# First-lane rows gathered two experts ahead, parts of an expert scattered without order, conditional rows gathered at the head of their block

## The chip, the core and the metric

The kernel runs on one core of a Trainium2 chip. The time is microseconds on the device for one execution. The engines of the core are TensorE (PE: matrix products and transposes), VectorE (DVE), ScalarE (ACT), GpSimd (POOL), which also issues the indirect transfers, and SyncE (SP), which issues the weight loads. Each has its own queue of instructions, and they wait for each other and for transfers by semaphores.

## The reference

One transformer layer on 2048 tokens of width 512, in float32: linear attention with a causal running state (16 heads, 4 key heads), then a mixture of experts. Only the experts matter here.

```
logits = xf @ w_cls.T;  scores = softmax(logits)            # 64 choices, 32 of them experts
topk_idx = top_k(scores + bias, 8)
w = 1.5 * scores[topk_idx] / sum(scores[topk_idx])
buf[e, pos] = xf of the tokens that chose expert e           # at most 256 for each
g, u = split(buf @ w_gate_up[e])                             # 512 -> 2 x 256
y = (silu(g) * u) @ w_down[e]                                # 256 -> 512
out[token] = sum over its experts of w * y                   # and a factor for the other choices
x = x + out
```

## The kernel before

**Attention.** Four blocks of 512 tokens. As each chunk of 128 tokens is finished, it is written to the output (`out<-x`), and its normalized row with its 32 expert weights to a table in memory, `rows`. `route` finds the eight choices, and `list_further` writes token numbers into `slots` by indirect transfers.

**Places.** `place` sorts the experts by the number of their tokens so far into eight groups of four. The eight fullest are the first lane of the groups: numbers 0, 4, 8, ..., 28. Rank r and place are tied by `place_of`.

**Three kinds of expert work.** A token list is cut at 32 and at 160 rows.

- *Groups.* The first 32 rows of the four experts of a group are one tile of 128 rows (`xg_b`). `group_up(q)` forms the gate and up products (L722), `group_down(q)` the down product (L739, `y_b` at L742), then a product that adds up equal rows (L744) gives `z` (L746), which is scattered.
- *First lane.* `over(4q, ...)` treats the next 128 rows (`xg_o`) and the last 96 rows (`xg_t`) of the group's first expert always: transposes (L708), gate and up products (L765), `aT` (SiLU on ScalarE L768, product on VectorE L769), down product (L778), and the weighted rows `y` (first part on ScalarE L786, second on VectorE L784). `weight` finds each row's weight on VectorE (`one` L687, `w` L689) from the gathered row itself.
- *Further experts.* After the last group, `further(r)` goes through the other ranks as nested blocks that run only while a flag says that the rank has more than 32 rows; a second flag adds 96 rows (`xg_r`).

**Gathers and scatters** are indirect transfers issued by GpSimd: `gather` (L675) takes rows by index from `rows`; `scatter` (L694) adds rows of 2 KB to the output. `tc.chain_iter_dep("out", ...)` puts every scatter in one chain. GpSimd issues a scatter of the chain when the one before has landed, and what stands behind it in GpSimd's queue waits as well.

**The loop over the groups:**

```
    gather_first(0)
    for q in range(NQ):
        if q + 1 < NQ:
            gather_first(q + 1)
        over(Q * q, [(xg_o[q % 2], P), (xg_t[q % 2], M2)])
        ...group_down(q), group_up(q + 1), two weight loads
```

`load_pair` loads the weights of two experts (3 MB) five pairs ahead, on SyncE, into buffers that come free when the products of earlier experts are done.

**Order.** The instructions are written for a scheduler that decides the order on each engine when the program is built, from its own estimate of when each operand is there; the order is then fixed. `tc.issue_after` keeps what it encloses behind one instruction on that engine's queue. The buffers of a tile (`bufs`) bound how far the scheduler can bring work forward.

Of the kernel before, what the change touches and what calls it, by code (L numbers as in the profile page):

```python
# [9 lines left out]
F32 = mybir.dt.float32  # L10
# [8 lines left out]
P = 128  # L19
S = 2048  # L20
# [9 lines left out]
E = 32  # L30
# [3 lines left out]
Q = 4  # L34
NQ = E // Q
# [11 lines left out]
XW = D + E  # L47
LATE = NQ - 2
# [19 lines left out]
def linattn_moe(  # L68
# [15 lines left out]
    nc = tc.nc  # L84
# [91 lines left out]
    def load_pair(i):  # L176

        home = units if i % 5 < 3 else more_units[0]
        tag = "unit" if home is units else "more"
        vs = [nc.values_load(eids[0:1, n : n + 1], engines=[mybir.EngineType.SP], min_val=0, max_val=E - 1,  # L180
                             skip_runtime_bounds_check_because="places hold a permutation of the experts")
              for n in (2 * i, 2 * i + 1)]
        for n, v in zip((2 * i, 2 * i + 1), vs):
            gu = home.tile([P, KD, 2, FI // P, P], F32, tag=tag, name=f"gu_{n}")
            nc.sync.dma_start(out=gu.rearrange("p k a c f -> p k (a c f)"),
                              in_=wgu[bass.ds(v, 1)].rearrange("e (k p) f -> p (e k) f", p=P))
            weights[n] = gu
        dn = home.tile([P, 2, FI // P, D], F32, tag=tag, name=f"dn_{i}")
        for j, v in enumerate(vs):
            nc.sync.dma_start(out=dn[:, j], in_=wdn[bass.ds(v, 1)].rearrange("e (k p) f -> p (e k) f", p=P))  # L190
            weights[2 * i + j] = weights[2 * i + j], dn[:, j]

    def list_further(ch, ai):

# [11 lines left out]
    with ExitStack() as ph:  # L206
# [335 lines left out]
        for sb in range(NSB):  # L542
            last = sb == NSB - 1
            if not last:
                blocks[sb + 1] = load_block(sb + 1)
            for g in range(G):
                if g == 0:
                    vas = [values(sb, c, xTs[sb]) for c in range(NC)]
                if g + 1 < G:
                    projs[sb, g + 1] = project(sb, g + 1, xTs[sb])  # L550
                elif not last:
                    xTs[sb + 1] = norm_block(sb + 1)
                    projs[sb + 1, 0] = project(sb + 1, 0, xTs[sb + 1])
                if last and g == 1:
                    rank_e = place()
                if last and g == G - 1:
                    for i in range(2):
                        load_pair(i)
                oT = otp.tile([P, R, SB], F32, tag="oT", name=f"oT_{sb}_{g}")
                oTs[sb, g] = oT  # L560
                for c in range(NC):
                    attend(sb, g, c, projs[sb, g], vas[c], oT)
                    if g == G - 1:
                        if c != 1 and waiting:
                            route_and_list(*waiting.pop(0))
                        if c >= 1:
                            waiting.append((sb * NC + c - 1,
                                            output(sb, c - 1, [oTs[sb, i] for i in range(G)])))
            listed = []
            if last:  # L570
                rows_so_far()
            xw = output(sb, NC - 1, [oTs[sb, i] for i in range(G)],
                        (lambda: listed.append(route(*waiting.pop(0)))) if last else None)
            with tc.issue_after(rstd_of.last.ins):
                for one in listed:
                    list_further(*one)
            while waiting:
                route_and_list(*waiting.pop(0))
            if last:
                route(sb * NC + NC - 1, xw)  # L580
            else:
                waiting.append((sb * NC + NC - 1, xw))
# [47 lines left out]
    def more(i, r):  # L630

        return (words[2 * i + r // 16] >> (r % 16)) & 1


    xg_b = [xgp.tile([P, XW], F32, name=f"xg_b{i}") for i in range(NQ)]
    xg_o = [xgp.tile([P, XW], F32, name=f"xg_o{i}") for i in range(2)]
    xg_t = [xgp.tile([P, XW], F32, name=f"xg_t{i}") for i in range(2)]
    xg_n = [xgp.tile([P, XW], F32, name=f"xg_n{i}") for i in range(3)]
    xg_r = xgp.tile([P, XW], F32, name="xg_r")
    for t in xg_o + xg_t + xg_n + [xg_r]:  # L640
        nc.scalar.mul(t, ident[:, 0:1].to_broadcast([P, XW]), 0.0)

    nc.vector.scalar_tensor_tensor(idx_f, held[:, :, 1], float(P), held[:, :, 0], ALU.mult, ALU.add)
# [27 lines left out]
    def column(n, i):  # L671
        return idx[:, i * E + n : i * E + n + 1]
# [11 lines left out]
    def weight(xg, k, what, of, name):  # L684

        one = xep.tile([P, E], F32, tag="one", name=f"one_{name}")
        nc.vector.scalar_tensor_tensor(one[:k], what, of, xg[:k, D:], ALU.is_equal, ALU.mult)  # L687
        w = xep.tile([P, 1], F32, tag="w", name=f"w_{name}", bufs=4)
        nc.vector.tensor_reduce(w[:k], one[:k], AX.X, ALU.add)  # L689
        return w  # L690

    def scatter(y, i):

        one = nc.gpsimd.indirect_dma_start(  # L694
            out=out,
            out_offset=bass.IndirectOffsetOnAxis(ap=i, axis=0),
            in_=y,
            in_offset=None,
            bounds_check=S - 1,
            oob_is_err=False,  # L700
            compute_op=ALU.add,
        )
        tc.chain_iter_dep("out", one.ins)

    def transposed(n, xg, xeT, m):
        pt = q_tr.tile([P, KD, P], F32, tag="tr", name=f"pe_{n}")
# [24 lines left out]
    def group_down(q, acts):  # L731
        py = q_y.tile([P, D], F32, tag="y", name=f"py_b{q}")
        for c, act in enumerate(acts):
            pa = q_ta.tile([P, P], F32, tag="ta", name=f"pa_{q}_{c}")
            nc.tensor.transpose(pa, act, ident)
            aT = xep.tile([P, P], F32, tag="aT_b", name=f"aT_b{q}_{c}")
            nc.scalar.copy(aT, pa)
            for j in range(Q):
                nc.tensor.matmul(py[ts(j, SL), :], lhsT=aT[:, ts(j, SL)], rhs=weights[Q * q + j][1][:, c, :],  # L739
                                 start=(c == 0), stop=(c == NF - 1))  # L740
        y = yp.tile([P, D], F32, tag="y_b", name=f"y_b{q}", bufs=2)
        nc.vector.tensor_copy(y, py)  # L742
        ps = q_y.tile([P, D], F32, tag="y", name=f"ps_{q}")
        nc.tensor.matmul(ps, lhsT=same[:, q, :], rhs=y, start=True, stop=True)  # L744
        z = yp.tile([P, D], F32, tag="z", name=f"z_{q}", bufs=2)
        nc.scalar.copy(z, ps)  # L746
        scatter(z, idx_s[:, q : q + 1])


    def over(e, parts):  # L750
# [24 lines left out]
        for c in range(NF):  # L775
            at = 0
            for py, (xg, k) in zip(pys, parts):
                nc.tensor.matmul(py[:k, :], lhsT=aTs[c][:, at : at + k], rhs=weights[e][1][:, c, :],  # L778
                                 start=(c == 0), stop=(c == NF - 1))
                at += k  # L780
        for i, (py, (xg, k)) in enumerate(zip(pys, parts)):
            y = yp.tile([P, D], F32, tag="y", name=f"y_{n}_{i}")
            if i:
                nc.vector.tensor_scalar(y[:k], py[:k], ws[i][:k], None, ALU.mult)  # L784
            else:
                nc.scalar.mul(y[:k], py[:k], ws[i][:k])  # L786
            scatter(y[:k], column(e, i)[:k])

    for i in range(2, AHEAD_W):
        load_pair(i)  # L790
# [24 lines left out]
    nc.vector.tensor_copy(idx, pi)  # L815

    def gather_first(q):
        gather(xg_o[q % 2], column(Q * q, 0), S)
        gather(xg_t[q % 2], column(Q * q, 1), S)

    def number_of(r):
        q, j = place_of(r)
        return Q * q + j

    def gather_rank(r):
        gather(xg_n[r % 3], column(number_of(r), 0), S)

    def reload(n, r):

# [8 lines left out]
    def further(r):  # L838

        n = number_of(r)  # L840
        with tc.If(more(0, r)):  # L841
            if n // Q < LATE:
                reload(n, r)
            with tc.If(more(1, r)) as cond:  # L844
                gather(xg_r, column(n, 1), S)
                over(n, [(xg_n[r % 3], P), (xg_r, M2)])
            with cond.Else():
                over(n, [(xg_n[r % 3], P)])
            if r + 3 < E:
                gather_rank(r + 3)  # L850
            if r + 1 < E:
                further(r + 1)

    gather_first(0)
    for q in range(NQ):
        if q + 1 < NQ:
            gather_first(q + 1)
        over(Q * q, [(xg_o[q % 2], P), (xg_t[q % 2], M2)])
        if ahead:
            group_down(q, ahead)  # L860
            ahead = None
        if FIRST <= q + 1 < NQ:
            ahead = group_up(q + 1)
        for i in range(2 * q, 2 * q + 2):
            if i + AHEAD_W < E // 2:
                load_pair(i + AHEAD_W)
# [54 lines left out]
```

## Time and profile before

| what | value |
|---|---|
| three timed runs, median | 1152.19 us (1149.51 to 1156.85) |
| the profiled execution, its own time | 1156.0 us |
| span of the profiled execution | 1154.3 us |
| mean granted TensorE clock | 0.96 |
| busy: TensorE, VectorE, ScalarE, GpSimd | 1036.8, 608.4, 209.8, 229.5 us |
| gathers xg_o and xg_t, each | 8 |
| gathers xg_n (further experts) | 6, of which three were used |
| scatters of y, of z | 19, 8 |
| start of the down product of experts 8, 12, 16, 20, 24, 28 | 992.12, 1017.79, 1042.55, 1066.52, 1089.57, 1108.17 us |
| last scatter, last gather | 1138.32, 1141.01 us |

The span runs from the first to the last instruction; the execution's own time adds what lies around it. "Granted clock" is the share of full speed that TensorE was given. A line of the timeline gives the start, the duration, the engine, the source line, the operation, out<-in, the count, and in brackets the engine's idle time just before with what ended it. An indirect transfer's duration on GpSimd is the time to issue it; it lands later, and the landing is seen where another instruction waits for it.

### The profile page before, as it was taken

The numbers are of one execution on the slowest core, as the hardware profiler recorded it, in microseconds if no ns is written. First come the engines' busy times: TensorE is split into PE (matmuls) and PEld (weight loads), VectorE is DVE, ScalarE is ACT, GpSimd is POOL, SyncE is SP. The second block draws the span as 40 slices with busy tenths as digits, with TensorE's granted clock in tenths as the row PEclk, the third lists the DMA queues.
The fourth block names the chain that finished last, engine by engine and source line by source line (L and its number), as shares of the span: only waits on it lengthen the run. The fifth ranks groups of instructions, "written<-read, shape, count | busy, mean of one in ns | idle before, by whom it ended". The sixth has DMA issues, their size and how long they took to land. (4 is left out here: it accounts for less than half of the span.)

```text
span 1154.3 us, 12767 instructions
## 1 busy us (share of the span) xinstructions
PE 1036.8 (90%) x4420; PEld 585.2 (51%) x4420; DVE 608.4 (53%) x1661; ACT 209.8 (18%) x543; POOL 229.5 (20%) x290
## 2 busy tenths in 40 slices
PE   6999899999998999999899999999897468888883
PEld 3455455544556554456455544556543326455452
DVE  4778874337885832678765426776434322222220
ACT  1122221001223200122222001223101010111110
POOL 6000000530000052300003331000241634222322
PEclk9999999999999999999999999999898588899997
DMA  9400000010000000100000000041004776999210
GB/s 349 151 1 1 18 1 10 30 65 0 1 8 12 11 29 19 56 1 1 1 1 20 29 29 0 1 182 37 19 30 144 289 242 187 344 321 331 27 20 6
DMA packets 51805, 87.25 MB, mean 76 GB/s; under 512 B 11342, under 2 KB 11470, under 8 KB 51728
## 3 DMA queue, kind: packets, MB, share of 16 engines
q1 hardware_dynamic: 35248, 67.31, 16.3%
q0 software_dynamic: 10720, 10.08, 4.1%
q10 hardware_dynamic: 5760, 8.92, 2.1%
q8 instruction: 38, 0.62, 0.2%
q14 instruction: 39, 0.32, 0.1%
HBM read 75.92 MB, written 15.88 MB: 80 GB/s over the span
## 5 line engine op out<-in xcount | busy, mean ns | idle before, releaser
L378 PE MATMUL px<-wo,oT 128*128 128x512 f32 x512 | 234.4, 602 | 0.0
L320 PE MATMUL pq<-xT,wq 128*128 128x512 f32 x512 | 230.5, 595 | 0.5 <-DVE rb_q L302 0.4
L196 POOL DMA_INDIRECT slots<-tok,ai x120 | 117.4, 979 | 242.5 <-DVE ai L478 210.2
L320 PEld LDWEIGHTS pq<-xT,wq 128*128 128x128 f32 x512 | 93.4, 191 | 106.6 <-issue 91.8
L378 PEld LDWEIGHTS px<-wo,oT 128*128 128x128 f32 x512 | 94.4, 194 | 97.7 <-issue 97.5
L342 PE MATMUL po<-va,at 128*128 128x129 f32 x512 | 99.5, 280 | 12.1 <-DVE at L335 11.8
L351 ACT ACTIVATE osb<-po,den 128x128 f32<-128x128 f32 x256 | 77.9, 365 | 152.0 <-DVE den L349 85.7
L342 PEld LDWEIGHTS po<-va,at 128*128 128x128 f32 x512 | 80.1, 193 | 35.7 <-DVE at L335 21.9
L345 PE MATMUL po<-state,qT 128*128 128x129 f32 x480 | 93.7, 277 | 0.0
L291 POOL MEMSET va<- 128x4 f32 x16 | 1.5, 110 | 415.5 <-PE pst L358 415.5
L345 PEld LDWEIGHTS po<-state,qT 128*128 128x128 f32 x480 | 73.6, 194 | 1.3 <-DVE state L361 0.8
L367 PE MATMUL pot<-ident,osb 128*128 128x128 f32 x256 | 60.7, 301 | 15.0 <-ACT osb L351 13.8
L305 ACT ACTIVATE rb_q<-rb_q 128x512 f32<-128x512 f32 x64 | 40.3, 630 | 179.3 <-DVE rb_q L304 164.1
L381 DVE TENSOR_TENSOR x<-px,xs 128x512 f32<-128x512 f32 x16 | 11.1, 692 | 108.9 <-PE px L378 60.6
L333 PE MATMUL psc<-qT,kT 128*128 128x512 f32 x128 | 68.2, 615 | 0.0
L367 PEld LDWEIGHTS pot<-ident,osb 128*128 128x128 f32 x256 | 35.9, 145 | 63.1 <-ACT osb L351 50.2
L765 PE MATMUL pu<-xeT,gu 128*128 128x224 f32 (+1 forms) x352 | 63.3, 339 | 3.9 <-DVE xeT L709 3.9
L765 PEld LDWEIGHTS pu<-xeT,gu 128*128 128x128 f32 x352 | 60.0, 194 | 6.0 <-ACT y L786 2.2
L313 PE MATMUL pk<-xT,wk 128*128 128x512 f32 x128 | 61.1, 614 | 0.8 <-ACT xT L280 0.7
L335 DVE TENSOR_TENSOR at<-psc,causal 128x512 f32<-128x512 f32 x64 | 44.0, 687 | 32.0 <-PE psc L333 31.9
L368 DVE COPY oT<-pot 128x512 f32<-128x512 f32 x64 | 43.9, 686 | 26.1 <-PE pot L367 26.0
L288 PE MATMUL pv<-wv,xT 128*128 128x512 f32 x128 | 57.0, 595 | 0.0
(223 smaller groups left out, 1207.5 us busy)
## 6 DMA issues: line engine op xcount, KB each, us to landing
gu<-in_wgu_dram SPq DMA_DIRECT2D x32, 1024.0 KB
dn<-in_wdn_dram SPq DMA_DIRECT2D x32, 512.0 KB
rows<-xw ACTq DMA_DIRECT2D x16, 272.0 KB
wq<-in_wqT_dram SPq DMA_DIRECT2D x4, 1024.0 KB
wo<-in_woT_dram SPq DMA_DIRECT2D x4, 1024.0 KB
out_dram<-x ACTq DMA_DIRECT2D x16, 256.0 KB
xs<-in_x_dram SPq DMA_DIRECT2D x3, 1024.0 KB
slots<-tok,ai POOLq DMA_INDIRECT x120
```

Source lines behind the costliest of these rows:

```text
L196: nc.gpsimd.indirect_dma_start(out=slots[k][:, :], out_offset=bass.IndirectOffsetOnAxis(ap=ai[:, k : k + 1], axis=0), in_=tok[:, ch : ch + 1],
L288: nc.tensor.matmul(pvf, lhsT=xT[:, k, ts(c, P)], rhs=wv[:, k, :], start=(k == 0), stop=(k == KD - 1))
L313: nc.tensor.matmul(pk, lhsT=wk[:, k, ts(g, HD)], rhs=xT[:, k, :], start=(k == 0), stop=(k == KD - 1))
L320: nc.tensor.matmul(pq, lhsT=wq[g][:, k, ts(r, HD)], rhs=xT[:, k, :], start=(k == 0), stop=(k == KD - 1))
L333: nc.tensor.matmul(psc, lhsT=kT[:, cc], rhs=qT[:, :, cc], start=True, stop=True)
L335: nc.vector.tensor_tensor(at, psc, causal.unsqueeze(1).to_broadcast([P, R, P]), ALU.mult)
L342: nc.tensor.matmul(po[:, i, :], lhsT=at[:, r, :], rhs=va[:, g, :], start=True, stop=(old is None))
L345: nc.tensor.matmul(po[:, i, :], lhsT=qT[:, r, cc], rhs=old, start=False, stop=True)
L351: nc.scalar.mul(osb[:, 2 * j + i, :], po[:, i, :HD], den[:, i : i + 1])
L367: nc.tensor.transpose(pt[:, r, :], osb[:, r, :], ident)
L378: nc.tensor.matmul(px, lhsT=oTs[h // R][:, h % R, ts(c, P)], rhs=wo[h // R][:, h % R, :], start=(h == 0), stop=(h == H - 1))
L765: nc.tensor.matmul(pu[:, a, :m], lhsT=weights[e][0][:, k, a, c, :], rhs=xeT[:, k, :m], start=(k == 0), stop=(k == KD - 1))
```

## The change

First-lane rows are gathered two groups ahead into three buffers. The two parts of a first-lane expert are collected and scattered together: both are made to wait for the scatters written before them, and not for each other; further experts keep the chain. Each conditional block gathers the rows of the rank three further on at its head and not at its end; two of the first-lane buffers serve there as the third and fourth buffer, and one as `xg_r`. The tile `w` has eight buffers in place of four. `rows_so_far` is queued behind the first weight loads.

```diff
-                    for i in range(2):
-                        load_pair(i)
+                    loaded = [load_pair(i) for i in range(2)][-1]
...
-                rows_so_far()
+                with tc.issue_after(loaded.ins):
+                    rows_so_far()
...
-    xg_o = [xgp.tile([P, XW], F32, name=f"xg_o{i}") for i in range(2)]
-    xg_t = [xgp.tile([P, XW], F32, name=f"xg_t{i}") for i in range(2)]
-    xg_n = [xgp.tile([P, XW], F32, name=f"xg_n{i}") for i in range(3)]
-    xg_r = xgp.tile([P, XW], F32, name="xg_r")
+    xg_o = [xgp.tile([P, XW], F32, name=f"xg_o{i}") for i in range(3)]
+    xg_t = [xgp.tile([P, XW], F32, name=f"xg_t{i}") for i in range(3)]
+    xg_n = [xgp.tile([P, XW], F32, name=f"xg_n{i}") for i in range(2)]
...
-        w = xep.tile([P, 1], F32, tag="w", name=f"w_{name}", bufs=4)
+        w = xep.tile([P, 1], F32, tag="w", name=f"w_{name}", bufs=8)
...
-    def scatter(y, i):
-
+    written = []
+
+    def scatter(ys, apart=True):
+        ones_ = [add_rows(y, i) for y, i in ys]
+        for one in ones_:
+            if not apart or not written:
+                tc.chain_iter_dep("out", one)
+            if apart:
+                for name in written:
+                    tc.add_manual_dep(one, name, mybir.DependencyInfo(mybir.DependencyClass.Sync,
+                                                                      mybir.DependencyReason.DATA),
+                                      reason="rows of the output are added to in turn")
+        written[:] = [one.name for one in ones_]
+        return ones_
+
+    def add_rows(y, i):
         one = nc.gpsimd.indirect_dma_start(
...
-        tc.chain_iter_dep("out", one.ins)
+        return one.ins
...
-            scatter(y[:k], column(e, i)[:k])
+            ys.append((y[:k], column(e, i)[:k]))
+        scatter(ys, e % Q == 0)
...
-        gather(xg_o[q % 2], column(Q * q, 0), S)
-        gather(xg_t[q % 2], column(Q * q, 1), S)
+        gather(xg_o[q % 3], column(Q * q, 0), S)
+        gather(xg_t[q % 3], column(Q * q, 1), S)
+
+    xg_n += [xg_o[LATE - 1 - 3], xg_t[LATE - 1 - 3]]
+    xg_r = xg_o[LATE - 6]
...
         with tc.If(more(0, r)):
+            if r + 3 < E:
+                gather_rank(r + 3)
             if n // Q < LATE:
                 reload(n, r)
...
-            if r + 3 < E:
-                gather_rank(r + 3)
             if r + 1 < E:
                 further(r + 1)
...
-    gather_first(0)
+    for q in range(2):
+        gather_first(q)
     for q in range(NQ):
-        if q + 1 < NQ:
-            gather_first(q + 1)
-        over(Q * q, [(xg_o[q % 2], P), (xg_t[q % 2], M2)])
+        if q + 2 < NQ:
+            gather_first(q + 2)
+        over(Q * q, [(xg_o[q % 3], P), (xg_t[q % 3], M2)])
```

More of the change, by code (lines that the diff above doesn't have):

```diff
@@ L189, in load_pair @@
         for j, v in enumerate(vs):
-            nc.sync.dma_start(out=dn[:, j], in_=wdn[bass.ds(v, 1)].rearrange("e (k p) f -> p (e k) f", p=P))
+            last = nc.sync.dma_start(out=dn[:, j], in_=wdn[bass.ds(v, 1)].rearrange("e (k p) f -> p (e k) f", p=P))
             weights[2 * i + j] = weights[2 * i + j], dn[:, j]
+        return last
     def list_further(ch, ai):
@@ L635, in linattn_moe @@
     xg_b = [xgp.tile([P, XW], F32, name=f"xg_b{i}") for i in range(NQ)]
-    xg_o = [xgp.tile([P, XW], F32, name=f"xg_o{i}") for i in range(2)]
-    xg_t = [xgp.tile([P, XW], F32, name=f"xg_t{i}") for i in range(2)]
-    xg_n = [xgp.tile([P, XW], F32, name=f"xg_n{i}") for i in range(3)]
-    xg_r = xgp.tile([P, XW], F32, name="xg_r")
-    for t in xg_o + xg_t + xg_n + [xg_r]:
+    xg_o = [xgp.tile([P, XW], F32, name=f"xg_o{i}") for i in range(3)]
+    xg_t = [xgp.tile([P, XW], F32, name=f"xg_t{i}") for i in range(3)]
+    xg_n = [xgp.tile([P, XW], F32, name=f"xg_n{i}") for i in range(2)]
+    for t in xg_o + xg_t + xg_n:
         nc.scalar.mul(t, ident[:, 0:1].to_broadcast([P, XW]), 0.0)
@@ L746, in group_down @@
         nc.scalar.copy(z, ps)
-        scatter(z, idx_s[:, q : q + 1])
+        one, = scatter([(z, idx_s[:, q : q + 1])])
+        if q == NQ - 1:
+            tc.chain_iter_dep("out", one)
     def over(e, parts):
@@ L780, in over @@
                 at += k
+        ys = []
         for i, (py, (xg, k)) in enumerate(zip(pys, parts)):
@@ L825, in gather_rank @@
     def gather_rank(r):
-        gather(xg_n[r % 3], column(number_of(r), 0), S)
+        gather(xg_n[r % 4], column(number_of(r), 0), S)
     def reload(n, r):
@@ L845, in further @@
                 gather(xg_r, column(n, 1), S)
-                over(n, [(xg_n[r % 3], P), (xg_r, M2)])
+                over(n, [(xg_n[r % 4], P), (xg_r, M2)])
             with cond.Else():
-                over(n, [(xg_n[r % 3], P)])
-            if r + 3 < E:
-                gather_rank(r + 3)
+                over(n, [(xg_n[r % 4], P)])
             if r + 1 < E:
                 further(r + 1)
-    gather_first(0)
+    for q in range(2):
+        gather_first(q)
     for q in range(NQ):
-        if q + 1 < NQ:
-            gather_first(q + 1)
-        over(Q * q, [(xg_o[q % 2], P), (xg_t[q % 2], M2)])
+        if q + 2 < NQ:
+            gather_first(q + 2)
+        over(Q * q, [(xg_o[q % 3], P), (xg_t[q % 3], M2)])
         if ahead:
```

## The prediction

> **What bounds the kernel now.** I start at the page: the span, the occupancy in slices and the memory traffic.
>
> ```profile
> span 1154.3 us, 12767 instructions
> ...
> PE   6999899999998999999899999999897468888883
> ...
> PEclk9999999999999999999999999999898588899997
> DMA  9400000010000000100000000041004776999210
> ```
>
> A slice is 28.9 us. Up to slice 31 (about 890 us) TensorE is at 9 tenths; that is attention, which the change does not touch. From slice 32 on TensorE is at 8 while the DMA row rises to 9: the experts. In the timeline there, an expert of the first lane starts its down product (L778) at 992.12, 1017.79, 1042.55, 1066.52, 1089.57 and 1108.17 us: periods of 25.7, 24.8, 24.0, 23.1 and 18.6. So the shortest period shows what TensorE needs, and the others lose 4.5 to 7.1 us each. The next view is TensorE's timeline in one long period and in the short one.
>
> ```profile
> 1021.32 1.93 PE L739 MATMUL py_b<-dn,aT_b 128*32 128x512 f32 x16
> 1023.06 1.03 PE L722 MATMUL pu_b<-gu,xeT_b 128*32 128x256 f32 x10
> 1028.51 1.84 PE L744 MATMUL ps<-y_b,same 128*128 128x512 f32 x2 [4.42 <-DVE y_b L742]
> 1030.28 4.14 PE L722 MATMUL pu_b<-gu,xeT_b 128*32 128x256 f32 x54
> ...
> 1095.83 1.13 PE L744 MATMUL ps<-y_b,same 128*128 128x512 f32 x2
> 1096.89 3.22 PE L722 MATMUL pu_b<-gu,xeT_b 128*32 128x256 f32 x54
> ```
>
> The bracket is idle time and what ended it. TensorE waits 4.42 us for the copy y_b on VectorE, and then runs slower. VectorE's timeline tells why y_b is late.
>
> ```profile
> 1021.43 0.75 DVE L784 TENSOR_SCALAR y<-py,w 96x512 f32<-96x512 f32 x1
> 1027.34 0.19 DVE L687 SCALAR_TENSOR_TENSOR one<-rank,xg_o 128x32 f32<-128x32 f32 x1 [5.17 <-DMA xg_o<-rows,idx]
> ...
> 1027.78 0.68 DVE L742 COPY y_b<-py_b 128x512 f32<-128x512 f32 x1
> ```
>
> The weight of the next expert (one, L687) stands ahead of y_b in VectorE's order and waits for that expert's gathered rows. GpSimd's timeline shows why the rows are late.
>
> ```profile
> 1000.81 1.61 POOL L694 DMA_INDIRECT out_dram<-y,idx  x1 [3.39 <-DMA out_dram<-y,idx]
> 1010.33 1.46 POOL L694 DMA_INDIRECT out_dram<-y,idx  x1 [7.91 <-issue]
> 1017.84 1.55 POOL L694 DMA_INDIRECT out_dram<-z,idx_s  x1 [6.05 <-issue]
> 1019.69 1.07 POOL L675 DMA_INDIRECT xg_o<-rows,idx  x1 [0.30 <-PE py L778]
> 1021.07 1.03 POOL L675 DMA_INDIRECT xg_t<-rows,idx  x1 [0.31 <-issue]
> 1025.88 1.62 POOL L694 DMA_INDIRECT out_dram<-y,idx  x1 [3.77 <-DMA out_dram<-z,idx_s]
> ```
>
> Each scatter is issued only when the one before it has landed: 9.5, 7.5, 8.0 us apart. Three of them make a period of some 24 to 25 us, and the gathers stand behind the third. So **the chain of scatters on GpSimd is the bound** from 970 to 1070 us, and TensorE follows it through gather, one and y_b. Once the weight loads are over (DMA share 0.24 at 1070 to 1075) the three take 10.1 us (1074.40 to 1084.51) and the period falls to 18.6.
>
> **The change, part by part.** I read it with the order of the instructions in both built programs and the semaphores that they wait for.
>
> *Parts without order.* The diff drops the order between the two parts of an expert. In the changed program the second part still waits for the semaphore that the first part's landing raises: the order on the output tensor is kept by the compiler's own tracking. So no scatter leaves the chain: 0 us. Had it gone, a period would lose one link of about 8 us.
>
> *Gathers.* GpSimd's order in the steady part is the same in both: part 0, part 1, z, two gathers, part 0. Only what is gathered differs: expert 4(q+3) instead of 4(q+2) behind z of group q-1. The two gathers that are added ahead of the first y scatter (about 1.3 us each, as at 958.87) stand where two gathers of further experts stood. Cost 0.
>
> *Where VectorE waits.* This decides. Before, the weight of the next expert stood behind y (L784) and ahead of y_b. In the changed program it is the weight of the expert after, but moved forward:
>
> ```
> xeT_b<-pe_b
> one_2_0<-rank,xg_o   (expert 20, third buffer, waits for its gather)
> aT_2_0<-aT,pu        (expert 8)
> aT_2_1<-aT,pu        (expert 8)
> ```
>
> The rows are wanted a period later, but the wait is now earlier, ahead of the gate products aT that the running expert's down product needs. The same stands for expert 24 ahead of aT of 12, and 28 ahead of aT of 16; for the later groups no first-lane gather is left. Behind the waiting instruction on VectorE stand aT, y, y_b and act_b; TensorE's L778 waits for aT, ScalarE's y for L778, the next scatter for y. So a loop closes: gather, aT, down product, part 0, part 1, z, next gather.
>
> Its links, for P = start of L778:
> - P to issue of part 0: 3.74 us (1089.57 to 1093.31).
> - TensorE has idled before P and runs slowly: after the 5.09 us of idle time at 954.87 the granted clock is 0.50 to 960 and 0.95 after, so 5 us at half speed, 2.5 us lost. Bounds 1.0 and 2.7 (the second as ps 0.94 plus pu_b 1.76 over the rows of 1095.83, after 4.27 us of idle time).
> - Part 0 to z: 15.8, 16.2, 17.0, 16.3, 18.3 us under loads, 10.1, 8.6, 7.7 without.
> - z to the gather's issue 1.85 (1017.84 to 1019.69).
> - Gather to one: 6.20, 7.65, 7.27 under loads, 3.21 without (1071.15 to 1074.36).
> - one 0.19, aT 0.39 and the hand-over: 0.7 to P.
>
> The step at expert 8: its gather (now 20) is behind part 1 of expert 4, issued at 995.01 and landed at 1001.21, both in the row as it is, since nothing differs before. P8 = 1001.21 + 0.7 = 1001.9 instead of 992.12. Part 0 at 1001.9 + 3.74 + 2.5 = 1008.1.
> The step at expert 12: TensorE's stall also holds back loads, since buffers come free at its products; but they follow in a burst at about 1010, so I take 16.0 for part 0 to z: z at 1024.1, gather at 1026.0, landed after 6.7 at 1032.7, P12 = 1033.4 (before 1017.79).
> The step at expert 16: part 0 at 1039.6. By then half of the time is free of loads, so 13.0 and 5.5: z 1052.6, gather 1054.5, landed 1060.0, P16 = 1060.7 (before 1042.55).
> Then no gather waits: P20 = 1060.7 + 18.6 + 2.5 = 1081.8, P24 = 1100.4, P28 = 1119.0, against 1108.17: **+10.8 us**. The old stalls at y_b are gone in this sum, since the 18.6 has none. The scatters keep up: z of expert 16 at about 1081, next ones unloaded.
>
> *Conditional rows at the block's head.* Three further experts run in this profile. Their gathers already stood ahead of need. What goes is the last gather behind the last scatter (1141.01 us, 1.08 us, behind 1.13 of idle time): 2.2 us off the end, between 0 (the end may wait for the scatter's landing) and 3.3 (the gather's landing counts in part). I take 2.2. At the head the gather goes past part 0's scatter on GpSimd's queue; there GpSimd waits 3.77 us (at 1124.95) for z to land, which hides its 1.1. If that cover were gone, it would cost 1.1 for each of three experts. The borrowed buffers come free with expert 20, long before.
>
> *Loads ahead of rows_so_far, eight buffers of w, eight zeroed tiles:* SyncE's order is unchanged, ScalarE zeroes eight tiles in both: 0; bounds plus or minus 1.
>
> **A rule against the row.** The Trainium skill, "DMA: Bandwidth & Descriptors", section "Anatomy of one DMA — SWDGE (gpsimd) path", gives about 2.0 us plus bytes over 436 GB/s for one DMA; an estimate from it for 128 rows of 2 KB is 2.6 us, where the trace has 8.1 us under loads. By that page the new loop would close in under 15 us, TensorE would set 18.6 in every period, and the time would fall by the 4.5 to 7.1 us of four periods, 23 us. The trace decides for the slow one.
>
> **Sum.** 10.8 - 2.2 = 8.6 us: a span of 1162.9 against 1154.3. The profiled run took 1156.0; the median of the three timed runs is 1152.2, 0.3% lower. Carried to the median: **1160.8**. About 1% (11.5 us) is what a measurement of this kernel can tell from no change.
>
> **The rivals.**
> 1. *Faster: the scatters speed up as soon as the stalled TensorE stops asking for weights.* For it: unloaded rows of 7.7 to 10.1 and a gather of 3.21. Against it: the loads come back in a burst right after each stall. With 14.0 and 5.0, then 9.0 and 3.2, and a loss of 1.0 per stall: P12 1028.2, P16 1047.8 (TensorE's 18.6 and 1.0), P28 1104.6, so -3.6, with up to 3.3 off the end and 1 from the rest 1144 on the median. Reaching 1130 needs in addition the stall at expert 8 to vanish, that is a gather landing by 992 in place of 1001.2: it decides from there, and nothing in the rows gives it. Chance 0.10.
> 2. *No change: the scatter chain sets about 24.5 us in both, the place of the wait does not matter.* For it: the chain was the bound. Against it: part 0 was ready 5 us before its turn (1045.9 against 1051.02), and the new loop adds a gather and a down product in series with two links. Then only the end moves: 1150 to 1152. Chance 0.17.
> 3. *Worse: loads stay dense all through,* 17.0 and 18.3 with gathers of 7.65: P12 1035.5, P16 1070.4, P28 1128.9, no gain at the end: 1173. Chance 0.13.
> 4. *The change does what it says* and the two parts leave together. The semaphore in the built program excludes it.
>
> **Numbers.** The forecast has 0.60, and within it the bounds run from 1153 to 1170, two fifths above 1163.7. Slower by over 1%: 0.24 + 0.13 = 0.37. Faster by over 1% (under 1140.7): 0.07, the tail of the first rival. The rest, 0.56, is within 1%. The range leaves out the faster tail and the top of rival 3: 1146 to 1172.
>
> **What would show it.** In the changed profile, one<-xg_o on VectorE must show its waits for the gather ahead of aT, not y_b; TensorE must idle some 9 us ahead of py (L778 as it was) three times and no longer ahead of ps; part 1 must still follow part 0 by a landing; three periods of 27 to 32 us, then 18.6. The prediction is wrong if TensorE's idle time ahead of py is under 3 us, or if the two parts leave 1.6 us apart.

## The result, and the profile after

The changed kernel takes 1161.53 us (median of 10 runs, 1155.02 to 1169.79), the kernel before beside it 1154.86 (10 runs): a ratio of **1.0073**, 95% interval 1.0052 to 1.0094. It is 0.7% slower, within the 1% that was set as no change. The ratio here and below is taken over all runs; the quotient of the two medians is a little smaller, 1.0058 (6.7 us). The profiled execution took 1163.65 us, the one of the kernel before 1156.0.

The page of the changed kernel, the span and the rows of the occupancy in 40 slices (now 29.0 us each):

```profile
span 1161.9 us, 12775 instructions
...
PE   6999899999989999999899999999887479678983
...
PEclk9999999999999999999999999999897679888997
DMA  9400000110000000100000000041006677697410
```

Counted from 0, slices 34 and 35 (988 to 1046 us) are the ones to look at: TensorE stands at 6 and 7 there, at 8 and 8 before. The DMA row has 6, 9, 7, 4 in slices 34 to 37 and 9, 9, 9, 2 before: a stalled TensorE frees buffers later, and the weight loads spread.

TensorE's timeline of the changed kernel, as one group follows the other (L796 is the down product py, L760 is ps):

```profile
1002.33 6.51 PE L796 MATMUL py<-dn,aT 128*128 128x512 f32 x8 [9.39 <-DVE aT L787]
...
1011.54 1.12 PE L760 MATMUL ps<-y_b,same 128*128 128x512 f32 x2
...
1031.67 5.50 PE L796 MATMUL py<-dn,aT 128*128 128x512 f32 x8 [7.58 <-DVE aT L787]
```

The stall has moved: nothing is left ahead of ps, and 9.39 and 7.58 us stand ahead of py. VectorE's timeline of the changed kernel says why (L687 is the weight of a later expert, L787 the gate product aT, L803 y, L758 y_b):

```profile
1001.79 0.19 DVE L687 SCALAR_TENSOR_TENSOR one<-rank,xg_o 128x32 f32<-128x32 f32 x1 [14.31 <-DMA xg_o<-rows,idx]
1001.90 0.68 DVE L787 TENSOR_TENSOR aT<-aT,pu 128x224 f32<-128x224 f32 x2
...
1008.88 0.75 DVE L803 TENSOR_SCALAR y<-py,w 96x512 f32<-96x512 f32 x1
...
1010.79 0.69 DVE L758 COPY y_b<-py_b 128x512 f32<-128x512 f32 x1 [0.66 <-PE py_b L755]
```

VectorE waits 14.31 us for a gather that expert 8 does not need, and both aT of expert 8 stand behind it. GpSimd's timeline of the changed kernel (L710 scatter, L675 gather) closes the loop:

```profile
994.39 1.08 POOL L675 DMA_INDIRECT xg_o<-rows,idx  x1 [0.30 <-issue]
...
1008.82 1.61 POOL L710 DMA_INDIRECT out_dram<-y,idx  x1 [12.01 <-ACT y L805]
1014.26 1.47 POOL L710 DMA_INDIRECT out_dram<-y,idx  x1 [3.83 <-issue]
1022.79 1.55 POOL L710 DMA_INDIRECT out_dram<-z,idx_s  x1 [7.07 <-issue]
1024.65 1.07 POOL L675 DMA_INDIRECT xg_o<-rows,idx  x1 [0.30 <-issue]
```

Part 0 is issued late (1008.82, since y is late), part 1 follows after 5.4 us and z after 8.5, and the next gather only then. Summed over 960 to 1120 us, the view of waits (total, times, longest) gives for the kernel before

```profile
DVE one L687 <- DMA xg_o<-rows,idx: 18.5, 5, 5.2
...
PE ps L744 <- DVE y_b L742: 15.9, 5, 4.4
```

and for the changed kernel

```profile
DVE one L687 <- DMA xg_o<-rows,idx: 42.2, 5, 14.3
...
PE py L796 <- DVE aT L787: 22.2, 4, 9.4
```

In what follows P0 and P28 are the starts of the down products of experts 0 and 28. P0 to P28 took 143.1 us before (965.12 to 1108.17) and 151.1 after (964.92 to 1116.01): 8.0 us more, where the span grew by 7.6. From P28 to the end it is 46.1 and 45.9 us.

### The profile page after: what moved, and what is told of

Its sections match the earlier page's. It is cut to its first block, busy times and chain, and to the rows that moved or that the text cites. A ratio compares the mean times of both kernels' runs of the same rounds, so it can differ in the third digit from the quotient of the medians.

```text
span 1161.9 us, 12775 instructions
## 1 busy us (share of the span) xinstructions
PE 1036.3 (89%) x4420; PEld 585.9 (50%) x4420; DVE 607.7 (52%) x1661; ACT 209.9 (18%) x543; POOL 230.0 (20%) x290
## 5 line engine op out<-in xcount | busy, mean ns | idle before, releaser
L796 PE MATMUL py<-dn,aT 128*128 128x512 f32 (+1 forms) x76 | 42.4, 707 | 22.2 <-DVE aT L787 22.2
L336 DVE TENSOR_TENSOR at<-psc,causal 128x512 f32<-128x512 f32 x64 | 43.9, 686 | 31.5 <-PE psc L334 31.3
```

The source lines that it names most:

```text
L336: nc.vector.tensor_tensor(at, psc, causal.unsqueeze(1).to_broadcast([P, R, P]), ALU.mult)
```

## The experiments

Theory 1 is the prediction's: VectorE's wait for a first-lane gather stands too early, and together with the scatters in series it makes a loop. Its rivals are named in the texts below. The first four runs were made on one chip, the others on a second one, on which the kernel before took 1147 to 1148 us and not 1155; each ratio is to the kernel before on the same chip. P0 to P28 is taken from the profile and leaves out what differs ahead of the experts.

| kernel | median us | ratio, 95% interval | P0 to P28 | P28 to end |
|---|---|---|---|---|
| before | 1154.9 | 1 | 143.1 | 46.1 |
| changed | 1161.5 | 1.007 (1.005 to 1.009) | 151.1 | 45.9 |
| changed, w in 4 buffers (a_w4) | 1142.7 | 0.988 (0.984 to 0.992) | 128.1 | 46.1 |
| before, w in 8 buffers (b_w8) | 1177.7 | 1.019 (1.015 to 1.023) | 165.5 | 46.4 |
| before, weight held back (b_late) | 1140.3 | 0.985 (0.982 to 0.989) | 128.2 | 46.2 |
| changed, parts really apart (a_apart) | 1146.5 | 0.993 (0.990 to 0.996) | 133.9 | 46.1 |
| w in 4, parts apart (a_w4_apart) | 1125.0 | 0.980 (0.975 to 0.985) | 120.2 | 45.8 |
| w in 4, y in 4 buffers (a_w4_y4) | 1133.5 | 0.989 (0.984 to 0.993) | 120.3 | 52.0 |
| before, weight held back, parts apart (b_late_apart) | 1128.0 | 0.983 (0.980 to 0.985) | 120.2 | 46.0 |
| before, gather at the head (b_head) | 1147.9 | 1.000 (0.999 to 1.002) | 142.8 | 46.1 |

### The buffers of w, undone in the changed kernel

```diff
-        w = xep.tile([P, 1], F32, tag="w", name=f"w_{name}", bufs=8)
+        w = xep.tile([P, 1], F32, tag="w", name=f"w_{name}", bufs=4)
```

> The changed kernel with four buffers of the tile w again, all else as changed. With that the scheduler puts the weight of expert 16 behind y of expert 8 and ahead of y_b of group 2, as before the change, while its rows are gathered a period earlier than before the change (behind z of group 0). Theory 1 (the place of VectorE's wait costs, not the gathers): VectorE no longer waits for a first-lane gather after 960 us, TensorE's idle time ahead of py falls from 9.4, 7.6, 4.6 us to under 2 each and none comes back ahead of ps; the scatters stay 8 us apart under loads, so TensorE gets ahead of them by what the y buffers allow (about 11 of the 22 us that it lost before), down product of expert 28 at about 1097, time 1141 to 1147. Rival A (the scatter chain sets the time, the place of the wait is irrelevant): 1152 to 1157, the stall turns up elsewhere. Rival C (another part of the change costs): 1160 or more.

Measured: 1142.7 us, P28 at 1095.95. The early wait is gone: over 960 to 1120 us VectorE waits 2.1 us in all for first-lane gathers (42.2 before this edit), and TensorE no longer idles ahead of py. The waits of this kernel in that stretch:

```profile
DVE one L687 <- DMA xg_o<-rows,idx: 2.1, 2, 1.2
```

One number in a tile of 128 x 4 bytes takes the ratio to the kernel before from 1.007 to 0.988. Rivals A and C are out. One detail of the expectation failed: a stall did come back ahead of ps, once, in the sixth period. Of this kernel, TensorE's timeline and then VectorE's:

```profile
1063.38 1.94 PE L760 MATMUL ps<-y_b,same 128*128 128x512 f32 x2 [4.67 <-DVE y_b L758]
```

```profile
1061.53 0.75 DVE L803 TENSOR_SCALAR y<-py,w 96x512 f32<-96x512 f32 x1 [5.44 <-DMA out_dram<-y,idx]
```

Here y of expert 20 waits for a buffer of y whose scatter has not yet landed: TensorE has run ahead of the chain as far as three buffers let it.

### The same number, alone, in the kernel before

```diff
-        w = xep.tile([P, 1], F32, tag="w", name=f"w_{name}", bufs=4)
+        w = xep.tile([P, 1], F32, tag="w", name=f"w_{name}", bufs=8)
```

> The kernel before with eight buffers of the tile w, nothing else changed: gathers one expert ahead, two buffers, chain of scatters and end as before. The scheduler then puts the weight of expert 16 ahead of aT of expert 8, and its gather stands behind z of group 1, as in the changed kernel. Theory 1: the same loop as in the changed kernel, TensorE idle 9, 8 and 5 us ahead of py and about 0 ahead of ps, down product of expert 28 some 8 us later than before, time 1160 to 1163. Rival A: 1152 to 1157. Rival C: no change, 1152 to 1157, since the cost sits in gathers, buffers or the end, which are as before.

Measured: 1177.7 us. The direction and the place are as theory 1 has them, the size is not. The waits of this kernel over 960 to 1120 us:

```profile
DVE one L687 <- DMA xg_o<-rows,idx: 54.7, 5, 14.5
...
PE py L778 <- DVE aT L769: 33.7, 5, 10.5
```

TensorE idles 10.49, 8.63, 5.48 and 8.11 us ahead of py: four rounds through the loop and not three. With gathers one group ahead the rows of expert 28 are still under way at expert 20, and the period from the down product of expert 16 to that of expert 20 is 30.0 us; in the changed kernel no gather is waited for there, and it is 21.4. From P0 to P28 this kernel is 14.4 us behind the changed one: 4.2 of them build up over the first three rounds, 8.5 come in the fourth. So **two parts of the change pull against each other**:

| ratio to the kernel before | w in 4 buffers | w in 8 buffers |
|---|---|---|
| gathers one group ahead | 1 | 1.019 |
| gathers two ahead, and the rest of the change | 0.988 | 1.007 |

### The weight held back in the kernel before

```diff
+    copied = {}
...
-        nc.vector.tensor_copy(y, py)
+        copied[q] = nc.vector.tensor_copy(y, py)
...
-        ws = [weight(xg, k, rank[:k], of, f"{n}_{i}") for i, (xg, k) in enumerate(parts)]
+        ws = []
+        if e % Q == 0 and e:
+            with tc.issue_after(copied[e // Q - 1].ins):
+                ws = [weight(xg, k, rank[:k], of, f"{n}_{i}") for i, (xg, k) in enumerate(parts)]
+        else:
+            ws = [weight(xg, k, rank[:k], of, f"{n}_{i}") for i, (xg, k) in enumerate(parts)]
```

> The kernel before, with the weight of a first-lane expert held on VectorE behind y_b of the group before it (so expert 12's behind y_b of group 2, whose rows were gathered behind z of group 0). Gathers, buffers and scatters as before. Theory 1: VectorE's waits of 4 to 5 us for gathers and TensorE's 4.4 us ahead of ps go; time as with the four buffers of w in the changed kernel, 1141 to 1147. Rival D (rows must be gathered two experts ahead for that): no gain, 1152 to 1157. Rival A: 1152 to 1157.

Measured: 1140.3 us, P0 to P28 128.2 us, the same as with gathers two groups ahead and four buffers of w. Rivals A and D are out: no earlier gather is needed, only a later place for the instruction that waits for it. Over 960 to 1120 us VectorE waits 1.1 us for first-lane gathers (18.5 before) and TensorE 5.7 us ahead of ps (15.9 before). The same single stall is left in the sixth period, since y waits for its buffer; VectorE's line, then TensorE's:

```profile
1060.34 0.75 DVE L791 TENSOR_SCALAR y<-py,w 96x512 f32<-96x512 f32 x1 [8.84 <-DMA out_dram<-y,idx]
```

```profile
1061.74 1.81 PE L746 MATMUL ps<-y_b,same 128*128 128x512 f32 x2 [4.93 <-DVE y_b L744]
```

### The two parts of an expert really apart

The changed kernel leaves the second part waiting for the first one's landing. This edit declares that dependency absent; an expert's list names a token once, so the two parts add to different rows.

```diff
+        if apart:
+            tc.declare_no_dep(ones_[-1], ones_[0], reason="two parts of one expert write different rows") if len(ones_) > 1 else None
         written[:] = [one.name for one in ones_]
```

> The changed kernel, with the dependency of an expert's second part on the first declared absent, so that in the built program part 1 no longer waits for part 0's landing; the early wait of VectorE stays. Theory 1: part 1 is issued some 1.6 us after y is ready or after part 0, not a landing later; a period has two links of about 8 us in place of three, part 0 to z falls from 14 to 9 us, the loop to about 24 us while loads run; TensorE still idles ahead of py, but 3 to 5 us less each; down product of expert 28 about 1102 to 1108, time 1147 to 1154. Rival E (two scatters together take as long as two in turn, because the transfer itself limits): part 0 to z stays 14, time 1159 to 1163.

Measured: 1146.5 us, a ratio of 0.993 where the changed kernel has 1.007. GpSimd's timeline:

```profile
1019.47 1.62 POOL L712 DMA_INDIRECT out_dram<-y,idx  x1 [10.03 <-ACT y L807]
1021.39 1.47 POOL L712 DMA_INDIRECT out_dram<-y,idx  x1 [0.30 <-issue]
1030.02 1.55 POOL L712 DMA_INDIRECT out_dram<-z,idx_s  x1 [7.16 <-DMA out_dram<-y,idx]
```

Part 1 leaves 1.9 us after part 0, and part 0 to z takes 9.2, 10.6 and 11.4 us at experts 8, 12 and 16, where it was 14.0, 10.8 and 13.9. VectorE still waits ahead of aT, but TensorE idles for it only at experts 12 and 16:

```profile
1014.01 5.32 PE L798 MATMUL py<-dn,aT 128*128 128x512 f32 x8 [2.96 <-DVE aT L789]
...
1038.52 6.71 PE L798 MATMUL py<-dn,aT 128*128 128x512 f32 x8 [3.94 <-DVE aT L789]
```

At expert 8 the gather that is waited for leaves at 984.70 and not at 994.39, and the down product starts at 992.10 and not at 1002.33. Rival E is out. P28 (1097.76) came below the expected 1102 to 1108, and the time just below 1147.

### Both causes away

The four buffers of w and the parts apart, in the changed kernel:

> The changed kernel with four buffers of w and with part 1 of an expert declared free of part 0: neither the early wait nor the third link in a period. Theory 1: with four buffers of w alone one stall is left (4.67 us ahead of ps, since y of expert 16 waits for a buffer that a scatter has not yet left); with two links a period, some 18 to 20 us, the scatters keep up, the stall goes and the periods are 18.6; down product of expert 28 at about 1090, time 1134 to 1139. Rival E (a pair of scatters takes as long as two in turn): the stall stays, time 1140 to 1144.

Measured: 1125.0 us, ratio 0.980. The expected times were worked out on the first chip; the ratio carried there gives about 1132, a little below the expected 1134. (The stall that the text puts at y of expert 16 is the one at y of expert 20 above.) From P0 to P28 it is 120.2 us:

```profile
957.64 3.60 PE L798 MATMUL py<-dn,aT 128*128 128x512 f32 x8
...
1077.88 3.60 PE L798 MATMUL py<-dn,aT 128*128 128x512 f32 x8
```

From expert 8 on every period is 18.6 or 18.7 us, with no stall ahead of py, and 0.81 us once ahead of ps. GpSimd's timeline:

```profile
1007.05 1.62 POOL L712 DMA_INDIRECT out_dram<-y,idx  x1 [4.49 <-ACT y L807]
1008.98 1.47 POOL L712 DMA_INDIRECT out_dram<-y,idx  x1 [0.30 <-issue]
1017.54 1.56 POOL L712 DMA_INDIRECT out_dram<-z,idx_s  x1 [7.09 <-DMA out_dram<-y,idx]
```

The pair takes 10.5 us, so rival E is out here too, and z has landed when the next part 0 is ready: the scatter at 1007.05 waited for ScalarE's y. The chain keeps step with TensorE, which is now the bound. A second set of runs of this kernel and of the one with four buffers of w alone, beside each other:

> The changed kernel with four buffers of w and parts apart once more, beside the other runs of this call: 120 us from the down product of expert 0 to that of expert 28, ratio to the kernel before 0.975 to 0.985.

> The changed kernel with four buffers of w once more, beside the other runs of this call: one stall of 4 to 5 us ahead of ps, 128 us from the down product of expert 0 to that of expert 28, ratio to the kernel before 0.985 to 0.991; some 8 us above the one with parts apart.

Measured: 1125.0 us, 0.981 (0.978 to 0.984), and 1136.3 us, 0.991 (0.989 to 0.994; stall 6.39 us ahead of ps, P0 to P28 128.3). Both miss a part of what was expected: the stall is longer than 5 us, and the medians are 11.2 us apart and not 8. Of the profiled runs 8.0 us lie between P0 and P28; 2.8 lie ahead of P0, where the two kernels do the same. So the order is worth some 8 us once the wait is late. This is the best kernel of the study, 2% under the kernel before.

### A fourth buffer of y in place of parts apart

In the changed kernel, with w in four buffers as above:

```diff
-    xg_n = [xgp.tile([P, XW], F32, name=f"xg_n{i}") for i in range(2)]
+    xg_n = [xgp.tile([P, XW], F32, name=f"xg_n{i}") for i in range(1)]
...
-    xg_n += [xg_o[LATE - 1 - 3], xg_t[LATE - 1 - 3]]
+    xg_n += [xg_o[LATE - 1 - 3], xg_t[LATE - 1 - 3], xg_t[LATE - 6]]
...
-            y = yp.tile([P, D], F32, tag="y", name=f"y_{n}_{i}")
+            y = yp.tile([P, D], F32, tag="y", name=f"y_{n}_{i}", bufs=4)
```

> The changed kernel with four buffers of w and four of y in place of three (xg_n has one tile of its own instead of two to make room, and borrows one more). Theory 1: the scatter chain stays three links of 8 us under loads, but TensorE gets one scatter further ahead of it; the 4.67 us ahead of ps and the slow products behind it go, periods 18.6 to 20, down product of expert 28 at about 1090, time 1134 to 1139. Rival A (the chain sets the end): no gain over the four buffers of w, 1140 to 1144.

Measured: the stall is gone and P0 to P28 is 120.3 us, as theory 1 has it; but the ratio is 0.989 (0.984 to 0.993), that of four buffers of w alone, as rival A has it. Of the 8 us gained, 6 are given back: P28 to the end takes 52.0 us and not 46. The end of GpSimd's timeline:

```profile
1106.61 1.57 POOL L710 DMA_INDIRECT out_dram<-y,idx  x1 [2.52 <-DMA out_dram<-z,idx_s]
...
1111.61 1.56 POOL L710 DMA_INDIRECT out_dram<-y,idx  x1 [1.06 <-DMA out_dram<-y,idx]
...
1116.03 1.57 POOL L710 DMA_INDIRECT out_dram<-y,idx  x1 [0.42 <-issue]
```

ScalarE finished the last y at 1109.38; its scatter is issued at 1116.03, 6.65 us later, because those ahead of it had to land one after the other. TensorE was freed, and **the chain itself set the end**.

### No weight loads

```diff
     def load_pair(i):
+        if i >= 5:
+            for n in (2 * i, 2 * i + 1):
+                weights[n] = weights[n - 10]
+            return
```

Both kernels with this edit compute experts 10 to 31 with other experts' weights.

> The kernel before without the weight loads of pairs 5 and up: experts 10 to 31 use the weights of the expert ten before (so the output is another). Theory 1, that scatters and gathers are slow because weight loads fill the DMA engines: scatters of the chain land in 4 to 5.5 us, VectorE waits for no gather, TensorE idles under 1 us ahead of ps, periods 18.6, time 1128 to 1136. Rival F (scatters are slow in themselves, 8 us): stalls as before, 1150 to 1157.

> The changed kernel without the weight loads of pairs 5 and up, as in the run beside it. Theory 1: VectorE's wait stands ahead of aT as in the changed kernel, but the loop has gather 3.2, 0.7, 3.7, part 0 to z some 9, 1.9 in it, together 18.5, no more than TensorE needs: stalls of 0 to 3 us, time 0 to 6 us above the run beside it. Rival F: stalls of 9, 8 and 5 us as with loads, 1158 to 1163.

Measured in one run each: 1116.8 and 1120.2 us. In the kernel before without loads VectorE waits for no first-lane gather over 960 to 1120 us, TensorE has P0 to P28 in 120.0 us, and the scatters follow each other in 4.7 to 5.7 us:

```profile
979.74 1.61 POOL L698 DMA_INDIRECT out_dram<-y,idx  x1 [5.55 <-ACT y L790]
985.45 1.46 POOL L698 DMA_INDIRECT out_dram<-y,idx  x1 [4.10 <-issue]
990.16 1.55 POOL L698 DMA_INDIRECT out_dram<-z,idx_s  x1 [3.25 <-issue]
```

Here part 0 to part 1 is 5.7 us and part 1 to z 4.7; with loads the same two links were 9.5 and 7.5: rival F is out. In the changed kernel without loads the early wait is still there, but little idle time is left ahead of py:

```profile
995.46 3.70 PE L800 MATMUL py<-dn,aT 128*128 128x512 f32 x8 [1.42 <-DVE aT L791]
1015.94 3.70 PE L800 MATMUL py<-dn,aT 128*128 128x512 f32 x8 [1.62 <-DVE aT L791]
```

It has 123.9 us from P0 to P28, 3.9 more than the run beside it; with loads the changed kernel has 23.0 more than with w in four buffers. So the early place costs little by itself and much with slow transfers. The second time lies 3.4 us above the first, as expected (0 to 6); the first lies below the expected 1128 to 1136. A part of that is ahead of the change: P0 was at 949.0 and 948.0, some 7 to 11 us earlier than in the runs with loads on that chip (956.4 to 959.3, once 963.9). The token numbers (idx) that the first gather needs were ready at 932.64 in the kernel before without loads, and at 942.89 with w in four buffers and the parts apart; P0 came 16.4 and 14.8 us later. That the loads slow the reads behind idx is likely, and was not tested by itself.

### Earlier gathers taken away again, with both causes gone

The kernel before with the weight held back and with the parts apart (the edits shown above):

> The kernel before (first-lane rows gathered one group ahead into two buffers, conditional rows at the block's end), with the weight of a first-lane expert held behind y_b of the group before, and with part 1 of an expert free of part 0. Theory 1 (the two causes are the place of the wait and the third link; the earlier gathers are worth nothing once the weight is late): 120 to 121 us from the down product of expert 0 to that of expert 28, no stall ahead of py or ps, time as the changed kernel with four buffers of w and parts apart, within 3 us of it, 0.975 to 0.985 of the kernel before. Rival D (rows must be gathered two groups ahead): some of the gain is missing, a stall ahead of pe, pu or ps, ratio 0.985 to 0.995.

Measured: 1128.0 us, 0.983 (0.980 to 0.985), P0 to P28 120.2 us, no stall ahead of py, and 0.81 us once ahead of ps. Beside 1125.0 us, 0.981 (0.978 to 0.984), the difference is within the intervals. Rival D is out: with the wait late, gathers two groups ahead are worth nothing that shows here.

### The gather at the block's head, alone

```diff
+    xg_n.append(xg_t[0])
+
     def gather_rank(r):
-        gather(xg_n[r % 3], column(number_of(r), 0), S)
+        gather(xg_n[r % 4], column(number_of(r), 0), S)
...
         with tc.If(more(0, r)):
+            if r + 3 < E:
+                gather_rank(r + 3)
...
-            if r + 3 < E:
-                gather_rank(r + 3)
...
```

> The kernel before, with the rows of a further rank gathered at the head of a conditional block (one borrowed tile as fourth buffer), nothing else changed. As predicted in the fifth step: no gather behind the last scatter, the span ends 2.2 us sooner after the down product of expert 28 (43.9 in place of 46.1 us). Rival G (the end is set by the landing of the last scatter and a fixed time behind it, a gather behind it lies beside that): 45.8 to 46.4 us, no change.

Measured: 46.1 us from P28 to the end, ratio 1.000 (0.999 to 1.002). The last instruction of GpSimd's timeline is now the scatter:

```profile
1129.93 1.57 POOL L694 DMA_INDIRECT out_dram<-y,idx  x1 [3.20 <-ACT y L786]
```

Rival G holds. In this kernel as in the one before, the last scatter is issued 30.2 us after P28, and the end comes 16.0 us later, whether a gather stands behind it (15.98 us) or not (15.97). What fills the 16.0 us is not shown.

## Why the prediction was right, and where it was not

The forecast was 1160.8 against 1161.5; as a ratio, to the 1152.2 us it started from, 1.0075 against 1.0073. Most views that it named show what it said: the wait ahead of aT, three stalls ahead of py and none ahead of ps, part 1 a landing behind part 0. Two did not come as said. The stalls are 9.39, 7.58 and 4.60 us and not some 9 three times. And of three periods of 27 to 32 us there is one: from expert 4 on the periods are 24.9, 29.3, 25.6, 21.4 and then 18.6; the prediction's own sum has only two in that range (31.5 and 27.3). So the mechanism was right, while the closeness of the sum is luck: a loss taken too large met a credit that was not there, and the cause was put in the wrong part of the change.

**The loop (step "Where VectorE waits"): mechanism right, two links mis-sized.**

| | predicted | measured |
|---|---|---|
| P8 | 1001.9 | 1002.33 |
| part 0, z of expert 8's round | 1008.1, 1024.1 | 1008.82, 1022.79 |
| P12 | 1033.4 | 1031.67 |
| part 0, z of expert 12's round | 1039.6, 1052.6 | 1037.32, 1048.16 |
| P16 | 1060.7 | 1057.23 |
| P28 | 1119.0 | 1116.01 |

The term that failed is part 0 to z: 16.0 and 13.0 were taken, 14.0 and 10.8 measured. The prediction argued that loads come back in a burst at about 1010 and keep the first link slow. The windows of the changed kernel (from:to, length, PE, PEld, DVE, ACT, POOL busy, granted clock, DMA share, GB/s) show a gap that part 0 fell into:

```profile
1000.00:1005.00 5.00, 2.67 (x3) 1.07 (x4) 0.79 (x3) 0.00 (x0) 0.00 (x0) 0.50 0.04 15
1005.00:1010.00 5.00, 5.00 (x18) 1.66 (x20) 1.27 (x5) 0.69 (x1) 1.18 (x1) 0.70 0.01 3
1010.00:1015.00 5.00, 5.00 (x66) 2.24 (x61) 1.18 (x3) 0.86 (x2) 1.17 (x2) 1.00 0.84 210
```

DMA share 0.04 and 0.01: at 1008.82 the first link began on idle DMA engines and took 5.4 us, the second, under the burst, 8.5. The gathers took 6.5 and 6.7 us (6.7 and 5.5 predicted), the slow clock cost py 2.9, 1.9 and 2.8 us (2.5 predicted, 3.60 being the full-speed time). Together the loop cost 7.8 us at P28 and not 10.8.

**The end (step "Conditional rows at the block's head"): wrong.** 2.2 us were credited; it gave 0.2, and alone nothing. The prediction's own lower bound, "the end may wait for the scatter's landing", was the case. 10.8 and -2.2 gave 8.6; the profile has 7.8 and -0.2. The good sum rests on two errors of opposite sign.

**The buffers of w (step "Loads ahead of rows_so_far, eight buffers of w"): the step that failed outright.** It priced them at 0, bounds plus or minus 1. They are the whole cause of the step that the prediction called decisive: the built order was read rightly, and its cost stands in the sum under "Where VectorE waits", but it was not traced to the line of the diff that made it. Alone they cost 1.9% (1.015 to 1.023), and without them the change is 1.2% faster than before.

**The gathers (step "Gathers"): priced at 0, and not 0.** GpSimd's order is indeed the same, but the rows that stand in it are wanted a group later, so with w in four buffers VectorE no longer waits for them. That was a gain which the moved wait ate. No run has the earlier gathers alone; the gain is read from the waits (2.1 us in place of 18.5). The prediction called the waiting weight that of the next expert before the change; counted by the gathers it is the one two groups on (expert 16 at expert 8), which is why holding it back one group was enough. In the changed kernel it is three groups on, expert 20 at expert 8, as the prediction's own lines have it.

**What bounds the kernel before: half right.** Three links of 8 us against 18.6 us of TensorE were there, but 1.5% went without touching the chain. The bound was a loop through gather, weight, y_b and ps, with the chain as a part of it; the chain alone came up only when that loop was cut, first through the buffers of y, then at the end.

**Parts without order: right.** 0 us, since part 1 still waited for part 0. "Had it gone, a period would lose one link of about 8 us" was too much: the pair takes 10.5 us and not 16 to 18, so 6 to 7 us go.

**The estimate of 2.6 us a scatter.** It came from the Trainium skill, "DMA: Bandwidth & Descriptors", section "Anatomy of one DMA — SWDGE (gpsimd) path"; no scatter in these runs shows such a time, neither with loads (7.5 to 9.5 us from one issue to the next in the kernel before) nor without (4.7 to 5.7). The nearest are second parts late in the run, 3.3 us (1116.30 to 1119.63 in the kernel before).

Rivals 1 and 3 of the prediction did not come (P12 1031.67 lies between their 1028.2 and 1035.5, the DMA gap is rival 1's mechanism at a part of its size: its 14.0 for the first part 0 to z is what was measured; its 9.0 for the second, 5.0 and 3.2 for the gathers and 1.0 for the slow clock are not). Rival 2, that the place of the wait does not matter, is refuted by the first two experiments.

## What to carry to other kernels

Where instructions are ordered by a scheduler, the number of buffers of even the smallest tile can decide how far its producer is brought forward, as that of w did here: compare the built order of each engine for every such number by itself, and ask of each instruction that waits for a transfer what stands behind it. An instruction that waits for a gather was best placed here behind all that does not need the gather. A dependency dropped in the source may be kept by the tracking of the tensor, so look for the semaphore, and measure what its absence is worth.

## What the runs showed of the hardware

- Two scatters issued 1.9 us apart overlap almost wholly: 10.5 us for the pair under weight loads, where one after the other took 16.4 and 17.9 (four buffers of w, part 0 to z at experts 12 and 8). The DMA engines were full in all three (share 1.03 to 1.07 by the view of windows).
- In the kernel before, the next link of the chain could follow a scatter of at most 128 rows of 2 KB after 4.7 to 5.7 us with a DMA share of 0.29 (970 to 1050 us, no loads) and after 7.5 to 9.5 with 0.96.
- TensorE ran slowly after 2.96 us of idle time (py 5.32 us, clock 0.77 in 1015 to 1020 with the parts apart), and not after 1.42 and 1.62 (py 3.70, clock 1.00). The Trainium skill, "TensorE: Matmul & The Clock Gate", Part 1, speaks of an idle window of about 3.4 us that runs freely. The 9.39 us of idle time here, with a clock of 0.50 after them, agree; the 2.96 us are shorter than the window and were followed by a slow clock all the same, though the profile models where a matmul ends.
